# Agent attention: scores laid out with pixels on partitions, one softmax shift for each half of the image

## Chip, cores and metric

The kernel runs on one core of a Trainium2 chip. The metric is the device time of one execution in microseconds (us); for the kernel before it is the median of three runs.

## The reference

Four residual layers act on `x` of shape 32 x 192 x 56 x 56, each on the group-normalised input. The first is the one that changes, an attention through 49 agents with 6 heads of 32 channels. For each image, with n = 3136 pixels:

```python
qkv = xf @ Wqkv + bqkv                       # q, k, v: n x 192
agent = q averaged over a 7 x 7 grid          # 49 x 192
agent_attn = softmax(agent @ k.T * scale + pos_bias, axis=pixels)   # per head: 49 x n
agent_v = agent_attn @ v                                            # per head: 49 x 32
q_attn = softmax(q @ agent.T * scale + agent_bias, axis=agents)     # per head: n x 49
out = (q_attn @ agent_v + depthwise_3x3(v)) @ proj_w + proj_b
```

The change concerns `agent_attn` and `agent_v`: a softmax over all pixels of an image, for each of 6 x 49 = 294 pairs of head and agent. The other three layers (a bidirectional WKV recurrence, a fractional shift, a long convolution through spectra) follow and are not touched.

## The kernel before

`all_blocks` first makes the filter of the last layer, then runs `attention` over the 32 images, then the WKV layer (`scan_pairs`) and the last two layers (`channel_blocks`). Everything is float32.

`attention` cuts an image into four pieces j = 0 to 3, strips of 16, 16, 16 and 8 columns (`WIDTHS`). A piece has two halves (upper and lower rows) of n = 448 pixels (224 in the last), which are again cut into `ns` = 4 (2) subs of 112 pixels (`SUB`). `xs_a` and `xs_c` hold the normalised channels of a piece with channels on partitions; rows 64 to 124 of `xs_c` hold constants that multiply the coefficients of the position bias, so that a score is two matmuls into one PSUM tile. `gk_a` and `gk_c` are the agents seen through the key weights (294 columns), `gq_a` and `gq_c` the same for the second softmax. All PSUM tiles of the attention come from one pool of four, of two banks each.

The work on an image, in the order of the program text:

1. For each piece: `weigh` computes the scores with agents on partitions, one tile of 98 x 2 x 448 for each of three pairs of heads (lines 659 and 660). VectorE takes the highest of a row, negated, into `low` (line 661), and ScalarE applies the exponential from PSUM into `pr` with that shift and adds up the denominators `sums` (line 663). `turn_v` transposes v on TensorE; `turn` transposes `pr` back to pixels on partitions into `prT` (lines 691 and 694), since the product with v sums over pixels. `gather` multiplies `prT` by v (line 706), and `settle` (lines 715 to 719) transposes that result to agents on partitions, into `got`. `find_v` and `convolve` (the depthwise convolution: one ScalarE instruction and eight VectorE instructions on each of two tiles, line 646) of later pieces stand between these. `moments` takes the statistics of the next image.
2. `join` brings the four pieces, each with its own shift, to one, divides by the denominators and yields `values`.
3. A loop over t works through the second softmax: `ask` (scores with pixels on partitions, lines 751 and 752; highest over the 49 agents, exponential, sum, division on VectorE and ScalarE, lines 755 to 768), `turn_back` (transposes, line 778), `answer` (line 791 onward), `project` (output weights and residual), with the next image's statistics, agents, first `find_v` and `convolve` between them. `ask(0)` stands before `join`, so that PE has work there.

A scheduler orders the instructions of each engine from this text, so the order on an engine can differ a little from it. Each engine then works strictly in its order. GpSimd (POOL) has nothing to do in the attention loop of the kernel before.

Of the kernel before, what the change touches and what calls it, by code (L numbers as in the profile page):

```python
# [20 lines left out]
F32 = mybir.dt.float32  # L21
I32 = mybir.dt.int32
AF = mybir.ActivationFunctionType
# [414 lines left out]
def attention(ctx: ExitStack, tc: tile.TileContext, a, ready, x1, st_a, st_c, beside):  # L438
# [15 lines left out]
    mm = nc.tensor.matmul  # L454
    UP, LOW = slice(0, 64), slice(64, 128)
    HALVES = ((0, UP), (1, LOW))
    P2 = slice(0, PAIR)

    def psum():
# [13 lines left out]
    gk_c, gq_c, xs_c = ready.gk_c, ready.gq_c, ready.xs_c  # L473

    NK = len(WIDTHS)
    xs_a = [cp.tile([128, S * w], F32, name=f"xs_a{j}", tag=f"xs_a{j}") for j, w in enumerate(WIDTHS)]


# [12 lines left out]
    def small(name, shape):  # L491
        return sp.tile(shape, F32, name=name, tag=name)
# [14 lines left out]
    def moments(x):  # L507

        st_a, st_c = small("st_a", [128, 7, 6]), small("st_c", [128, 4, 6])
        flat = [t.rearrange("p y x -> p (y x)") for t in x]  # L510
        for i in range(7):
            nc.vector.bn_stats(st_a[:, i], flat[0][:, i * 448 : (i + 1) * 448])
        for i in range(4):
            nc.vector.bn_stats(st_c[:, i], flat[1][:, i * 392 : (i + 1) * 392])
        mv = small("mv", [128, 2, 2])
        nc.vector.bn_aggr(mv[:, 0], st_a.rearrange("p a b -> p (a b)"))
        nc.vector.bn_aggr(mv[:, 1], st_c.rearrange("p a b -> p (a b)"))
        pool_a, pool_c = small("pool_a", [128, AG]), small("pool_c", [65, AG])
        by_x = [wp.tile([128, n, POOL], F32, name="by_x", tag=f"by_x{n}", bufs=1) for n in (S, S // 2)]
        for t in range(2):  # L520
            nc.vector.tensor_reduce(
                by_x[t].rearrange("p y q -> p (y q)"), x[t].rearrange("p y (q x) -> p (y q) x", x=8), AX.X, ALU.add
            )
        nc.vector.tensor_reduce(
            pool_a.rearrange("p (w q) -> p w q", w=POOL), by_x[0].rearrange("p (w y) q -> p w q y", y=8), AX.X, ALU.add
        )
        fours = small("fours", [64, 2 * POOL, POOL])
        for h, r in HALVES:
            nc.vector.tensor_reduce(
                fours[:, h * POOL : (h + 1) * POOL], by_x[1][r].rearrange("p (w y) q -> p w q y", y=4), AX.X, ALU.add  # L530
            )
        nc.vector.tensor_tensor(
            pool_c[0:64].rearrange("p (w q) -> p w q", w=POOL), fours[:, 0::2], fours[:, 1::2], ALU.add
        )
        nc.vector.memset(pool_c[64:65], 1.0)
        return mv, (pool_a, pool_c)
# [45 lines left out]
    def seen(ag, w, to_c, name):  # L582

        ps = psum()
        for i, cols in enumerate((slice(0, 128), slice(128, C + 1))):
            n = (128, 65)[i]
            mm(ps[:n, i, : 4 * AG], w[0][:, cols], ag[0], start=True, stop=True)
            mm(ps[:n, i, 4 * AG : HA], w[1][:, cols], ag[1], start=True, stop=True)
        g = small(name, [128, HA])
        nc.scalar.copy(g, ps[:, 0, :HA])  # L590
        c = sp.tile([65, HA], F32, name="once", tag="once", bufs=1)
        nc.scalar.copy(c, ps[0:65, 1, :HA])
        nc.sync.dma_start(out=to_c[0:65], in_=c.unsqueeze(1).to_broadcast([65, 2 * NK, HA]))
        return g
# [53 lines left out]
        return o  # L648


    def weigh(j, g, low, sums):
        _, n, _ = sizes(j)
        prs = []
        for p in range(3):
            cols = slice(p * PAIR, (p + 1) * PAIR)
            ps = psum()
            for h in range(2):
                px = slice(h * n, (h + 1) * n)
                mm(ps[P2, h, :n], g[:, cols], xs_a[j][:, px], start=True, stop=False)  # L659
                mm(ps[P2, h, :n], gk_c[0:KC, 2 * j + h, cols], xs_c[j][0:KC, px], start=False, stop=True)  # L660
            nc.vector.tensor_reduce(low[:, j, p : p + 1], ps[P2, :, :n], AX.XY, ALU.max, negate=True)  # L661
            pr = wp.tile([PAIR, 2, CH], F32, name="pr", tag="weights", bufs=5)
            nc.scalar.activation(  # L663
                pr[:, :, :n], ps[P2, :, :n], AF.Exp, bias=low[:, j, p : p + 1], accum_out=sums[:, j, p : p + 1]
            )
            prs.append(pr)
        return prs

    def turn_v(j, v):

# [8 lines left out]
            nc.scalar.copy(vT[:, s0 : s0 + 2], ps[:SUB, :, : 3 * 128])  # L679
        return vT  # L680

    def turn(j, prs):

        _, _, ns = sizes(j)
        prT = wp.tile([SUB, 8, HA], F32, name="prT", tag="turned", bufs=2)
        for q in range(0, 2 * ns, 2):
            ps = psum()
            for i in range(2):
                h, s = divmod(q + i, ns)
                for p in range(3):  # L690
                    nc.tensor.transpose(
                        ps[:SUB, i, p * PAIR : (p + 1) * PAIR], prs[p][:, h, s * SUB : (s + 1) * SUB], ident[P2, P2]
                    )
            nc.scalar.copy(prT[:, q : q + 2], ps[:SUB, :, :HA])
        return prT

    def gather(j, prT, vT):

        _, _, ns = sizes(j)
        ps = psum()  # L700
        for p in range(3):
            cols = slice(p * PAIR, (p + 1) * PAIR)
            for s in range(ns):
                for h, r in HALVES:
                    c = h * 128 + p * 64 if p < 2 else 256 + h * 64
                    mm(ps[r, 0, cols], vT[:, s, c : c + 64], prT[:, h * ns + s, cols], start=(s == 0), stop=(s == ns - 1))
        halves = wp.tile([128, HA], F32, name="halves", tag="halves", bufs=1)
        nc.scalar.copy(halves, ps[:, 0, :HA])
        return halves

# [10 lines left out]
    def join(low, sums, got):  # L721

        m = small("m", [PAIR, 3])
        nc.vector.tensor_reduce(m, low.rearrange("p j a -> p a j"), AX.X, ALU.min)
        f = small("f", [PAIR, NK, 3])
        nc.vector.tensor_tensor(f, m.unsqueeze(1).to_broadcast([PAIR, NK, 3]), low, ALU.subtract)
        nc.scalar.activation(f, f, AF.Exp)
        nc.vector.tensor_tensor(sums, sums, f, ALU.mult)
        den = small("den", [PAIR, 3])
        nc.vector.tensor_reduce(den, sums.rearrange("p j a -> p a j"), AX.X, ALU.add)  # L730
        nc.vector.reciprocal(den, den)
        nc.vector.tensor_tensor(f, f, den.unsqueeze(1).to_broadcast([PAIR, NK, 3]), ALU.mult)
        by_pair = got.rearrange("p j (a d) -> p (j a) d", a=3)
        nc.vector.tensor_tensor(
            by_pair, by_pair, _bc(f.rearrange("p j a -> p (j a)"), [PAIR, NK * 3, 2 * HD]), ALU.mult
        )
        values = small("values", [PAIR, 3, 2 * HD])
        nc.vector.tensor_reduce(values.rearrange("p a d -> p (a d)"), got.rearrange("p j c -> p c j"), AX.X, ALU.add)
        nc.vector.tensor_tensor(values, values, heads.unsqueeze(1).to_broadcast([PAIR, 3, 2 * HD]), ALU.mult)
        return values  # L740


    def ask(j, g):
        _, _, ns = sizes(j)
        pq = wp.tile([SUB, 8, HA], F32, name="pq", tag="turned", bufs=2)
        for q0 in range(0, 2 * ns, 4):
            for q in range(q0, q0 + 4, 2):
                ps = psum()
# [22 lines left out]
    def turn_back(j, pq):  # L771
        _, n, ns = sizes(j)
        out = []
        for p in range(3):
            ps = psum()
            for q in range(2 * ns):
# [1 line left out]
                nc.tensor.transpose(  # L778
                    ps[P2, h, s * SUB : (s + 1) * SUB], pq[:, q, p * PAIR : (p + 1) * PAIR], ident[:SUB, :SUB]
                )  # L780
            t = wp.tile([PAIR, 2, CH], F32, name="pqT", tag="weights", bufs=5)
            nc.scalar.copy(t[:, :, :n], ps[P2, :, :n])
            out.append(t)
        return out
# [43 lines left out]
    gk = seen(ag, wkT, gk_c, "gk_a")  # L828
    for j in range(NK):
        normed(nxt, rs, nb, j)  # L830
    v, o = {0: find_v(0), 1: find_v(1)}, {}
    o[0] = convolve(0)
    for b in range(NB):
        x, more = nxt, b + 1 < NB
        if more:
            nxt = ready.image(nc, a, b + 1)
        beside(b)
        low, sums = small("low", [PAIR, NK, 3]), small("sums", [PAIR, NK, 3])
        got = sp.tile([PAIR, NK, C], F32, name="got", tag="got", bufs=1)
        turned, asked, back = {}, {}, {}  # L840
        for j in range(NK):
            prs = weigh(j, gk, low, sums)
            if j == 0:
                gq = seen(ag, wqT, gq_c, "gq_a")
            vT = turn_v(j, v[j])
            if j > 0:
                halves = gather(j - 1, *turned[j - 1])
            if j + 2 < NK:
                v[j + 2] = find_v(j + 2)
            turned[j] = turn(j, prs), vT  # L850
            if j > 0:
                settle(j - 1, halves, got)
            if j + 1 < NK:
                o[j + 1] = convolve(j + 1)
            elif more:
                mv, pools = moments(nxt)
        halves = gather(NK - 1, *turned[NK - 1])
        asked[0] = ask(0, gq)
        settle(NK - 1, halves, got)
        values = join(low, sums, got)  # L860
        done, o = o, {}
        st = small("st", [128, 2, 9])
# [1115 lines left out]
```

## Time and profile before

| | us |
|---|---|
| median of 3 runs (10781.03 to 10796.38) | 10793.86 |
| time of the profiled execution | 10811.08 |
| span of the profiled execution | 10809.3 |
| `values` of the first and of the last image (start of its last instruction) | 278.1 and 4932.4 |
| busy over the span: PE, VectorE, ScalarE, POOL | 9604.3, 9260.0, 6372.8, 2918.0 |

The attention occupies roughly the first 5000 us. PE is TensorE's matmul, DVE is VectorE, ACT is ScalarE. A float32 matmul shows as two records, a transpose as one. A duration of a record includes its start and its way through the pipeline, so instructions that follow each other closely overlap by some 0.08 us on DVE; on PE the distance from start to start is the price of an instruction in a dense sequence.

### The profile page before, as it was taken

To read this page: it belongs to the slowest core of one execution; us is meant where nothing else is said; L and a number is where in the kernel's file an instruction comes from. 1 tells how busy PE (TensorE), PEld (TensorE's weight loads), DVE (VectorE), ACT (ScalarE), POOL (GpSimd) and SP (SyncE) were. 2 spreads that over 40 slices of the span, in tenths; PEclk is the share of its full clock that TensorE was granted. 3 is DMA by queue.
4 is the path that set the end of the run, shared out by engine and by line. 5 is a ranking of instruction groups with operands and counts; after the bars stand their busy time and mean duration, and the time that the engine had idled before them with its cause. 6 is when DMAs were issued, how large, how long until landed. Compare 5 with 4: busy or idle time off the path is not lost. (4 is left out here: it accounts for less than half of the span.)

```text
span 10809.3 us, 166766 instructions
## 1 busy us (share of the span) xinstructions
PE 9604.3 (89%) x64806; PEld 5959.0 (55%) x64806; DVE 9260.0 (86%) x11668; ACT 6372.8 (59%) x11964; POOL 2918.0 (27%) x2614
## 2 busy tenths in 40 slices
PE   6999999999999999998888888888888799999998
PEld 3555555555555555554333333333333577787876
DVE  5888888888888888887999999999999577777877
ACT  3555555555555555554666666666666466666766
POOL 0000000000000000002655555555555444444441
PEclk8999999999999999998999999999999899999999
DMA  4211221112121111111344333333444589999998
GB/s 122 63 47 49 63 64 63 37 58 63 64 63 35 61 46 46 46 34 56 92 102 98 97 97 97 97 97 97 97 101 103 153 269 273 274 275 273 278 274 264
DMA packets 1104877, 1240.31 MB, mean 115 GB/s; under 512 B 773091, under 2 KB 807200, under 8 KB 1091992
## 3 DMA queue, kind: packets, MB, share of 16 engines
q1 hardware_dynamic: 1083148, 1201.53, 38.8%
q10 hardware_dynamic: 20932, 28.02, 1.0%
q8 instruction: 516, 8.45, 0.3%
q14 instruction: 281, 2.30, 0.1%
HBM read 915.94 MB, written 306.43 MB: 113 GB/s over the span
## 5 line engine op out<-in xcount | busy, mean ns | idle before, releaser
L646 DVE SCALAR_TENSOR_TENSOR o<-v_a,att_w,o 128x896 f32<-128x896 f32 (+1 forms) x1024 | 1053.3, 1029 | 421.7 <-ACT v_a L620 296.6
L1163 POOL MEMSET f<- 128x1 f32 x96 | 8.8, 98 | 4842.7 <-DMA st_c<-st 4837.7
L1543 DVE STREAM_TRANSPOSE z<-turned 128x1792 f32<-128x1792 f32 x192 | 677.4, 3528 | 258.3 <-ACT turned L1543 257.8
L1543 ACT COPY y<-ps 64x252 f32<-64x252 f32 (+1 forms) x2304 | 784.0, 340 | 157.9 <-PE ps L1543 128.1
L1156 ACT ACTIVATE q<-q 128x784 f32<-128x784 f32 x384 | 328.3, 855 | 813.6 <-DVE q L1151 638.5
L663 ACT ACTIVATE pr<-ps,low 98x896 f32<-98x896 f32 (+1 forms) x384 | 352.3, 918 | 567.8 <-DVE low L661 567.8
L911 PE MATMUL ps<-sq,fixed 128*128 128x392 f32 x512 | 296.8, 742 | 427.7 <-ACT sq L1234 427.7
L764 ACT ACTIVATE pq<-pq 112x1176 f32<-112x1176 f32 x224 | 265.3, 1184 | 683.3 <-DVE pq L756 654.1
L751 PE MATMUL ps<-gq_a,xs_a 128*112 128x294 f32 x1792 | 609.0, 422 | 46.6 <-DVE pq L756 24.1
L1543 POOL TENSOR_TENSOR xn<-x,scale 128x896 f32<-128x896 f32 x192 | 328.4, 1711 | 1192.3 <-DMA x<-x 759.4
L646 DVE SCALAR_TENSOR_TENSOR o<-v_c,att_w,o 128x448 f32<-128x448 f32 (+1 forms) x1024 | 634.3, 619 | 7.5 <-ACT v_c L631 2.4
L659 PE MATMUL ps<-xs_a,gk_a 128*98 128x448 f32 (+1 forms) x1536 | 638.9, 497 | 0.0
L660 PE MATMUL ps<-xs_c,gk_c 125*98 125x448 f32 (+1 forms) x1536 | 631.3, 492 | 0.0
L911 PE MATMUL ps<-x,weights 128*128 128x392 f32 x1536 | 573.7, 516 | 31.1 <-DVE bv L1185 14.1
L752 PE MATMUL ps<-gq_c,xs_c 125*112 125x294 f32 x1792 | 581.4, 411 | 0.0
L1543 PEld LDWEIGHTS ps<-toep,y 128*32 128x32 f32 x16896 | 508.2, 151 | 113.4 <-ACT y L1543 109.2
L1543 PE MATMUL ps<-toep,y 128*32 128x112 f32 x16896 | 554.8, 287 | 0.0
L1543 PE MATMUL ps<-rows,xn 128*112 128x112 f32 x3072 | 378.5, 281 | 159.6 <-POOL xn L1543 136.0
L1543 ACT ACTIVATE turned<-ps,rs 128x448 f32<-128x448 f32 (+1 forms) x576 | 384.4, 668 | 203.4 <-PE ps L1543 195.7
L1543 PE MATMUL ps<-fixed,padded 128*128 128x168 f32 x3072 | 490.0, 314 | 0.0
L766 DVE TENSOR_REDUCE sm<-pq 112x24 f32<-112x1176 f32 x224 | 307.7, 1374 | 181.9 <-ACT pq L764 181.9
L1543 PEld LDWEIGHTS ps<-fixed,padded 128*128 128x128 f32 x3072 | 455.6, 195 | 2.4 <-issue 1.9
(367 smaller groups left out, 25548.6 us busy)
## 6 DMA issues: line engine op xcount, KB each, us to landing
toep<-spans SPq DMA_DIRECT2D x192, 2352.0 KB
x<-x SPq DMA_DIRECT2D x576, 392.0 KB
x<-x SPq DMA_DIRECT2D x896, 196.0 KB
out_x<-done SPq DMA_DIRECT2D x384, 196.0 KB
spans<-lags SPq DMA_DIRECT2D x24, 2352.0 KB
x<-in_x SPq DMA_DIRECT2D x32, 1568.0 KB
x<-x SPq DMA_DIRECT2D x32, 1568.0 KB
x<-in_x SPq DMA_DIRECT2D x64, 392.0 KB
```

Of the source, the lines that this page charges most:

```text
L646: nc.vector.scalar_tensor_tensor(dst, tap(i), dww[:, t, i : i + 1], dst, ALU.mult, ALU.add)
L659: mm(ps[P2, h, :n], g[:, cols], xs_a[j][:, px], start=True, stop=False)
L660: mm(ps[P2, h, :n], gk_c[0:KC, 2 * j + h, cols], xs_c[j][0:KC, px], start=False, stop=True)
L663: nc.scalar.activation(pr[:, :, :n], ps[P2, :, :n], AF.Exp, bias=low[:, j, p : p + 1], accum_out=sums[:, j, p : p + 1])
L751: mm(ps[:SUB, i, :HA], xs_a[j][:, px], g, start=True, stop=False)
L752: mm(ps[:SUB, i, :HA], xs_c[j][0:KC, px], gq_c[0:KC, 2 * j + (q + i) // ns], start=False, stop=True)
L764: nc.scalar.activation(flat, flat, AF.Exp)
L766: nc.vector.tensor_reduce(sm, rows, AX.X, ALU.add)
L911: mm(out, aa, srcs[t][h], start=True, stop=False)
L1156: nc.scalar.activation(den, den, AF.Ln)
L1163: nc.gpsimd.memset(s, 0.0)
L1543: return lambda *args, **kw: self.tc.keep_in_program_order(do(*args, **kw))
```

## The change

The scores of the first softmax are computed with pixels on partitions, as `ask` does for the second (`score`), and copied by ScalarE into SBUF tiles `sc` of 112 x 8 x 294 (4 x 294 for the last piece). These tiles have the memory that `prT` and `pq` had, now three of the large kind and one of the small. No transposes of exponentials are needed (`turn` is gone). The shift is now one for each half image (pieces 0 and 1, pieces 2 and 3): `highest` takes the maximum over the subs of two pieces on VectorE, `top` transposes that on TensorE and takes the maximum across what were partitions into `low`; `apart` is a diagonal form of it, and `lower` spreads it over 112 partitions with a matmul against ones, subtracts it from all scores of the half image on VectorE, in place, and takes the exponential on ScalarE, in place. `fold` adds the exponentials over subs on GpSimd into `side`, and `add_up` adds `side` over partitions with a matmul into `sums`. `gather` runs over two pieces in one accumulation, so that `settle` runs twice for an image and `join` works on two parts. `tops`, `side`, `halves` and the row sums of `moments` share the buffers of `pqT` (three in place of five).

The diff, cut to its core:

```diff
-    def weigh(j, g, low, sums):
...
-            for h in range(2):
-                px = slice(h * n, (h + 1) * n)
-                mm(ps[P2, h, :n], g[:, cols], xs_a[j][:, px], start=True, stop=False)
-                mm(ps[P2, h, :n], gk_c[0:KC, 2 * j + h, cols], xs_c[j][0:KC, px], start=False, stop=True)
-            nc.vector.tensor_reduce(low[:, j, p : p + 1], ps[P2, :, :n], AX.XY, ALU.max, negate=True)
...
-            nc.scalar.activation(
-                pr[:, :, :n], ps[P2, :, :n], AF.Exp, bias=low[:, j, p : p + 1], accum_out=sums[:, j, p : p + 1]
...
+    def score(j, g):
...
+        for q in range(0, 2 * ns, 2):
+            ps = psum()
+            for i in range(2):
+                px = slice((q + i) * SUB, (q + i + 1) * SUB)
+                mm(ps[:SUB, i, :HA], xs_a[j][:, px], g, start=True, stop=False)
+                mm(ps[:SUB, i, :HA], xs_c[j][0:KC, px], gk_c[0:KC, 2 * j + (q + i) // ns], start=False, stop=True)
+            nc.scalar.copy(sc[:, q : q + 2], ps[:SUB, :, :HA])
+        return sc
+    def highest(parts):
+        tops = wp.tile([SUB, 2, HA], F32, name="tops", tag="weights", bufs=WB)
+        for i, (j, sc) in enumerate(parts):
+            n = 2 * sizes(j)[2]
+            nc.vector.tensor_reduce(tops[:, i], sc[:, :n].rearrange("p q c -> p c q"), AX.X, ALU.max)
+        nc.vector.tensor_tensor(tops[:, 0], tops[:, 0], tops[:, 1], ALU.max)
+        return tops
+    def fold(parts):
...
+        nc.gpsimd.tensor_tensor(side[:, 0:2], t[:, q : q + 2], u[:, r : r + 2], ALU.add)
+        for t, q in rest[2:]:
+            nc.gpsimd.tensor_tensor(side[:, 0:2], side[:, 0:2], t[:, q : q + 2], ALU.add)
+        nc.gpsimd.tensor_tensor(side[:, 0], side[:, 0], side[:, 1], ALU.add)
+        return side
+    def top(i, side, low):
...
+            nc.tensor.transpose(ps[P2, 0, p * SUB : (p + 1) * SUB], side[:, 0, p * PAIR : (p + 1) * PAIR], ident[:SUB, :SUB])
+        nc.vector.tensor_reduce(
+            low[:, i], ps[P2, 0, : 3 * SUB].rearrange("p (a n) -> p a n", a=3), AX.X, ALU.max, negate=True
+        )
+        apart = sp.tile([PAIR, 3, PAIR], F32, name="apart", tag="apart", bufs=1)
+        nc.vector.tensor_tensor(
+            apart, ident[P2, P2].unsqueeze(1).to_broadcast([PAIR, 3, PAIR]), _bc(low[:, i], [PAIR, 3, PAIR]), ALU.mult
+        )
+        return apart
+    def lower(parts, apart):
+        ps = psum()
+        mm(ps[:SUB, 0, :HA], ones[P2, :SUB], apart.rearrange("p a b -> p (a b)"), start=True, stop=True)
+        for j, sc in parts:
...
+            nc.vector.tensor_tensor(
+                sc[:, :n], sc[:, :n], ps[:SUB, 0, :HA].unsqueeze(1).to_broadcast([SUB, n, HA]), ALU.add
             )
...
+            nc.scalar.activation(flat, flat, AF.Exp)
+    def add_up(i, side, sums):
+        ps = psum()
+        for p in range(3):
+            mm(ps[P2, 0, p : p + 1], side[:, 0, p * PAIR : (p + 1) * PAIR], ones[:SUB, 0:1], start=True, stop=True)
+        nc.vector.tensor_copy(sums[:, i], ps[P2, 0, 0:3])
...
-    def turn(j, prs):
...
+        sc[0] = score(0, gk)
+        gq = seen(ag, wqT, gq_c, "gq_a")
+        sc[1] = score(1, gk)
+        tops = highest([(j, sc[j]) for j in range(2)])
+        for j in range(2):
+            vT[j] = turn_v(j, v[j])
+        v[2] = find_v(2)
+        o[1] = convolve(1)
+        apart = top(0, tops, low)
+        sc[2] = score(2, gk)
+        lower([(j, sc[j]) for j in range(2)], apart)
+        v[3] = find_v(3)
+        o[2] = convolve(2)
+        sc[3] = score(3, gk)
+        side = fold([(j, sc[j]) for j in range(2)])
+        halves = gather([(j, sc[j], vT[j]) for j in range(2)])
+        add_up(0, side, sums)
+        tops = highest([(j, sc[j]) for j in range(2, 4)])
+        for j in range(2, 4):
+            vT[j] = turn_v(j, v[j])
+        settle(0, halves, got)
+        o[3] = convolve(3)
+        apart = top(1, tops, low)
         asked[0] = ask(0, gq)
-        settle(NK - 1, halves, got)
+        lower([(j, sc[j]) for j in range(2, 4)], apart)
+        if more:
+            mv, pools = moments(nxt)
+        side = fold([(j, sc[j]) for j in range(2, 4)])
+        halves = gather([(j, sc[j], vT[j]) for j in range(2, 4)])
+        add_up(1, side, sums)
+        settle(1, halves, got)
         values = join(low, sums, got)
```

## Prediction

> **What bounds the kernel now.** I read the busy shares, then the period of an image from the rows of `values`, then one image cut into two stretches. The last instruction of `values` starts at 278.1 in the first image and at 4932.4 in the last, so 31 periods take 4654.3 us, 150.1 us an image, 4803 us for 32. Only this part changes; the remaining 6000 us stay.
>
> ```profile
> PE 9604.3 (89%) x64806; PEld 5959.0 (55%) x64806; DVE 9260.0 (86%) x11668; ACT 6372.8 (59%) x11964; POOL 2918.0 (27%) x2614
> ...
> L739 DVE TENSOR_TENSOR values<-values,att_k x32: 282/346/352, 278.1 to 4932.4; 98x192 f32<-98x192 f32 x32
> ...
> core 0: us, PE busy (x) PEld busy (x) DVE busy (x) ACT busy (x) POOL busy (x), PEclk, DMA share, GB/s
> 2090.80:2157.60 66.80, 63.54 (x301) 37.36 (x301) 50.02 (x77) 41.55 (x67) 0.00 (x0) 0.92 0.05 10
> 2157.60:2241.70 84.10, 80.05 (x508) 51.39 (x506) 77.39 (x116) 39.56 (x78) 0.00 (x0) 1.00 0.28 94
> ```
>
> The two stretches are one image: from its predecessor's `values` to the first score matmul (stretch B, the loop over t), and from there to its own `values` (stretch A, where everything that the change touches lies). The reader should see that PE bounds both, and that in A DVE is close behind: 77.4 of 84.1 us. Whatever lightens PE there can win 6.7 us an image at most, and whatever adds more than that to DVE makes A longer even if DVE never waits.
>
> The groups of the attention, by form, over 28 images (500 to 4700 us), and the neighbours among them that price the new instructions:
>
> ```profile
> line engine op names shapes xcount | busy us, mean ns | idle before us <-releasers
> L661 DVE TENSOR_REDUCE low<-ps 98x1 f32<-98x896 f32 x252 | 268.6, 1084 | 6.6 <-PE ps L660 5.7
> L661 DVE TENSOR_REDUCE low<-ps 98x1 f32<-98x448 f32 x84 | 51.2, 610 | 0.0
> L766 DVE TENSOR_REDUCE sm<-pq 112x24 f32<-112x1176 f32 x196 | 269.2, 1374 | 162.1 <-ACT pq L764 162.1
> L738 DVE TENSOR_REDUCE values<-got 98x192 f32<-98x768 f32 x28 | 40.5, 1447 | 0.0
> L524 DVE TENSOR_REDUCE pool_a<-by_x 128x49 f32<-128x392 f32 x28 | 23.6, 843 | 0.0
> L768 DVE TENSOR_TENSOR pq<-pq,sm 112x1176 f32<-112x1176 f32 x196 | 269.4, 1374 | 1.6
> L764 ACT ACTIVATE pq<-pq 112x1176 f32<-112x1176 f32 x196 | 232.1, 1184 | 610.9 <-DVE pq L756 585.8 <-DVE f L732 24.3
> L694 ACT COPY prT<-ps 112x588 f32<-112x588 f32 x392 | 230.0, 658 | 12.8 <-PE ps L691 11.5
> ```
>
> L738 is the row to look at: it takes longer for 768 elements than L766 for 1176. Both are sums along the free dimension, but L766 reads neighbours, L738 steps 192 elements.
>
> **PE, per image.** From the timeline, a float32 matmul of 448 columns costs 0.755 us from start to start (2158.41, 2159.17, 2159.92), one of 224 0.38, one of 294 0.497, and 24 transposes of L691 2.2. Away go 36 x 0.755 + 12 x 0.38 = 31.7 of scores, 84 transposes of 0.093 = 7.8, and two `settle` of 0.4. In come 56 x 0.497 = 27.8 of scores, two spreading matmuls (1.0), six transposes of `tops` and six matmuls of `add_up` (together 1.6). The balance is -9.9 us, all in A: PE falls to 70 us there.
>
> **ACT, per image.** Fourteen copies of `prT` (0.66) become fourteen copies of `sc` of the same shape. Twelve exponentials with accumulator reads, 13.4 us, become four: L764 and L663 (896 elements, 1011 ns) give 0.83 ns an element behind 0.2 us, so 2.16 for 2352 elements and 1.2 for 1176, 7.7 together. Two `halves` and `got` copies go. ACT has half of A free, so the 7 us count for nothing; without that cover they would be a gain.
>
> **DVE, per image.** Away: L661 11.4 us (319.8 / 28), two additions of L719 (0.6), and half of L738 and of the scaling of `got` (1.05): 13.05. In come:
> - Four reductions of `highest`, over 8 (4) scores that lie 294 elements apart. Here a rule and a row differ. L738 and L524 (steps of 192 and 7) cost 1.69 and 1.77 ns an element behind 0.15 us; at 1.7, 2352 elements take 4.15 us and 1176 take 2.15: 14.3 for the image when 0.08 of overlap is taken off each. The Trainium skill, "VectorE: DVE Perf Modes", section "The perf-mode tier table", gives `tensor_reduce` one rate, 1x, with no condition on its step; its 0.96 GHz and L766's start give 2.6 and 1.38 us, so 8.8. I take the row; the rule would make the sum 5.5 us smaller. The other end is 2.15 ns an element (the dearest stepped row near, `fours` of 196 elements in 486 ns, start included), 3.5 us more.
> - Four additions of `lower` of 2352 and 1176 elements: L768 has 1176 in 1374 ns, so 2.6 and 1.37, 8.85 dense.
> - Two maxima of 294, two `apart`, two `low` (336 elements from PSUM), at 0.36, 0.36 and 0.42 dense, between L719 (192, 0.34) and L755 (588, 0.76); two tiny copies of `sums`: 2.5.
>
> 25.6 in, 13.05 out: +12.6. DVE needs 90.0 us in A where A lasted 84.1. PE's 9.9 us are therefore worth nothing, and DVE sets A.
>
> **Waits on DVE in A.** I walk the order of the changed program as built, with time 0 at the first score matmul. (1) Two pieces are scored before their maximum: 2 x 7.95 us with `seen` (1.6) between. DVE's remaining convolution and residual work of the image before ends at 6.7, the first piece is copied at 8.7, its reduction ends at 12.8; the second piece is copied at 18.3, and nothing stands between the two reductions on DVE. Waits 2.0 + 5.5 = 7.5 us. (2) Then DVE is dense: second reduction, statistics, thirteen taps with `low` and `apart`, the two `lower` additions to 43.5. PE waits for `apart`, and later for exponentials, which costs nothing. (3) In the second half image the order on DVE is `lower`, `lower`, one division by sums, then the copy of `sums`, then `join`. That copy waits for `add_up`, which waits for `fold` on POOL: six additions behind the first exponential. POOL's rows are 421 ns for 112 elements and 1692 for 896, so 1.19 + 0.08 between for 588, 0.8 for the last of 294: 7.15 us. From the end of the first addition: exponential 2.2, fold 7.15, PE 0.5, 9.9 us; DVE has 2.8 of work. Wait 7. Queued behind it are `join`, all `answer`s and `ask(1)`. On PE `ask(1)` stands behind `add_up` too. (4) The first fold (8 additions, 9.7 us) has 11.7 us of taps beside it on DVE, and would be hidden.
>
> **The lock.** Those taps read two operands from SBUF. What that does beside POOL shows in the last layers:
>
> ```profile
> L1543 DVE TENSOR_TENSOR padded<-x,mean x192: 1061/1081/2403, 8522.2 to 10734.8; 128x896 f32<-128x896 f32 x192
> ...
> L1543 POOL TENSOR_TENSOR xn<-x,scale x192: 1682/1692/2536, 8475.0 to 10662.3; 128x896 f32<-128x896 f32 x192
> ...
> L1150 POOL COPY f<-p 128x1 f32<-128x1 f32 x192 | 344.8, 1796 | 315.2 <-DVE p L1149 307.2
> ```
>
> Min, median, max: mostly the two miss each other, and then nothing is lost; where they meet, one takes 1.3 us longer. A copy of one column lasts 1.8 us on POOL beside DVE's two-operand scans. The median row alone would price the lock at nothing; the Trainium skill, "SBUF — State Buffer", section "Who interferes with whom", says that a DVE instruction with two SBUF inputs and a POOL instruction that reads SBUF exclude each other for a whole instruction, which speaks against this change: eight additions, 7 x 1.19 + 0.72 = 9 us of DVE standing still. The bounds are 0 and about 15 (POOL kept out until the taps end, then waited for); I take 9, since the maxima show whole instructions lost and the taps are dense.
>
> **Sum.** A: 90.0 + 7.5 + 7 + 9 = 113.5, +29.4 over 84.1. B stays bound by PE; `ask(1)` is computed after `add_up` and not before `values`, so B starts with PE some 2.5 us late (at most 5, at least 0). +31.9 an image, x 32 = +1021. Against the profiled execution: 10811 + 1021 = 11832; that execution was 17 us above the median, so 11815. No DMA is added or moved past another on SP's queue: `seen` still loads `gq_c` long before `ask(0)`. Three buffers for `pqT` in place of five cost nothing, as `answer` frees them on PE ahead of the next transposes; if a copy did wait, up to 1 us on each of four pieces.
>
> **Rivals.** *The lock costs nothing*: the first fold hides as in (4). A 104.5, +22.9 with B: x 32 = +733, 11527. For: the median row; against: its maximum. *POOL is kept out and stepped reads are dear*: +3.5 and +6 more, 41.4 an image, 12120. For: one copy in the scan took 3.55 us. *DVE reads at the contiguous rate and fills its waits*: 84.5 us in A; if the reductions overlap other work and POOL's sums arrive early, A is 84.5 or slightly less and the time is 10800, not slower; it turns at 84.1 us of DVE time and waits in A. If the waits in B shrank too by the 3 us PE has free there, 10700. For: the rule on `tensor_reduce`; against: L738, and a wait that the order as built contains. That the change doesn't do what it says is excluded by that order.
>
> **Numbers.** Main case with its spread 0.60, no lock 0.20, POOL kept out 0.13, not slower 0.07. A range of 11430 to 12120 leaves out about 2 in 10. 0.2% of this time, 22 us, is about what a measurement can tell from no change: faster by more 0.04, same 0.03, slower 0.93.
>
> **What would show it.** Reductions into `tops` of 4.15 us (2.6 would be the rule); `side` additions of 1.2 us in the second fold, longer in the first, and taps above 1.15 us beside them; DVE idle some 5.5 us before the second reduction and some 7 before the copy of `sums`, released by PE; PE busy about 73% in the attention; `values` every 182 us. A period under 160 us would make the walk wrong, one of 150 the whole argument.

## The result

The changed kernel takes 11951.42 us (median of four, 11944.33 to 11968.09) against 10795.12 us before (four, 10781.03 to 10803.1): a ratio of 1.1075, 95% interval 1.1056 to 1.1094. It is 1156 us slower where 1020 were forecast, and inside the range that was stated (11430 to 12120). The profiled execution has a span of 11947.9 us.

The profile after, in the views that the prediction used: the busy line of the page, the row of `values`, and one image cut in two (from its first score matmul to its `values`, A; from there to the next first score matmul, B; PEclk is the clock that TensorE was granted, 1.00 being full speed).

```profile
PE 9611.3 (80%) x63142; PEld 6121.3 (51%) x63142; DVE 9733.2 (81%) x11732; ACT 6224.5 (52%) x11196; POOL 3802.3 (32%) x3063
...
L781 DVE TENSOR_TENSOR values<-values,att_k x32: 357/358/359, 294.3 to 6068.2; 98x192 f32<-98x192 f32 x32
...
core 0: us, PE busy (x) PEld busy (x) DVE busy (x) ACT busy (x) POOL busy (x), PEclk, DMA share, GB/s
2437.30:2558.00 120.70, 77.89 (x430) 56.02 (x429) 91.16 (x118) 35.25 (x54) 27.42 (x14) 0.77 0.20 65
2558.00:2627.30 69.30, 67.30 (x329) 38.17 (x327) 51.45 (x78) 41.21 (x67) 0.00 (x0) 0.98 0.04 10
```

(6068.2 - 294.3) / 31 = 186.3 us an image, where it was 150.1. Nearly all of the loss is in A, 120.7 us for 84.1; B has 69.3 for 66.8. No engine is busy for 120 us in A: VectorE works 91.2 and stands for 29.5. What it stands for, first as a list of waits (total us, times, longest) between 500 and 5800 us, then in the order of one image, and under it GpSimd in the same stretch:

```profile
DVE sums L721 <- PE ps L720: 531.8, 49, 12.3
DVE tops L676 <- ACT sc L668: 204.7, 57, 5.5
...
2446.21 4.18 DVE L676 TENSOR_REDUCE tops<-sc 112x294 f32<-112x2352 f32 x1 [1.79 <-ACT sc L668]
2455.85 4.27 DVE L676 TENSOR_REDUCE tops<-sc 112x294 f32<-112x2352 f32 x1 [5.46 <-ACT sc L668]
2504.93 0.16 DVE L721 COPY sums<-ps 98x3 f32<-98x3 f32 x1 [12.30 <-PE ps L720]
2554.97 0.16 DVE L721 COPY sums<-ps 98x3 f32<-98x3 f32 x1 [9.33 <-PE ps L720]
...
2483.87 10.03 POOL L686 TENSOR_TENSOR side<-sc 112x588 f32<-112x588 f32 x1 [118.57 <-ACT sc L715]
2493.98 8.91 POOL L688 TENSOR_TENSOR side<-side,sc 112x588 f32<-112x588 f32 x6
2502.98 0.70 POOL L689 TENSOR_TENSOR side<-side 112x294 f32<-112x294 f32 x1
2545.17 1.75 POOL L686 TENSOR_TENSOR side<-sc 112x588 f32<-112x588 f32 x1 [41.49 <-ACT sc L715]
2547.01 5.94 POOL L688 TENSOR_TENSOR side<-side,sc 112x588 f32<-112x588 f32 x4
```

The wait ahead of `sums` is put down to PE, but PE only passes on what GpSimd finished 1.25 us earlier (2503.68). The same kind of addition takes 10.03 us at 2483.87 and 1.75 at 2545.17. The first of them starts inside VectorE's taps and ends 1.3 us after the last of those, about what one addition takes, and the taps beside it have their usual length:

```profile
2490.88 1.15 DVE L649 SCALAR_TENSOR_TENSOR o<-v_a,att_w,o 128x896 f32<-128x896 f32 x1
2491.94 0.69 DVE L649 SCALAR_TENSOR_TENSOR o<-v_c,att_w,o 128x448 f32<-128x448 f32 x1
2504.93 0.16 DVE L721 COPY sums<-ps 98x3 f32<-98x3 f32 x1 [12.30 <-PE ps L720]
```

In the last eight images, which have no `beside` copies, the scheduler puts `moments` behind the second `lower`. The second wait is covered there and the period is 179 us, where it is 189 in the mean of the images before. The trace thus holds a first test by itself.

### The profile page after: what moved, and what is told of

Read it like the earlier page. It is cut to its first block, busy times and chain, and to the rows that moved or that the text cites. A ratio compares the mean times of both kernels' runs of the same rounds, so it can differ in the third digit from the quotient of the medians.

```text
span 11947.9 us, 163456 instructions
## 1 busy us (share of the span) xinstructions
PE 9611.3 (80%) x63142; PEld 6121.3 (51%) x63142; DVE 9733.2 (81%) x11732; ACT 6224.5 (52%) x11196; POOL 3802.3 (32%) x3063
## 5 line engine op out<-in xcount | busy, mean ns | idle before, releaser
L686 POOL TENSOR_TENSOR side<-sc 112x588 f32<-112x588 f32 x64 | 377.2, 5894 | 4995.1 <-ACT sc L715 4995.1
L649 DVE SCALAR_TENSOR_TENSOR o<-v_a,att_w,o 128x896 f32<-128x896 f32 (+1 forms) x1024 | 1064.4, 1039 | 238.1 <-ACT o L647 129.4
L793 PE MATMUL ps<-gq_a,xs_a 128*112 128x294 f32 x1792 | 696.1, 480 | 103.2 <-DVE low L697 103.1
L676 DVE TENSOR_REDUCE tops<-sc 112x294 f32<-112x2352 f32 (+1 forms) x128 | 471.7, 3708 | 225.3 <-ACT sc L668 225.3
L649 DVE SCALAR_TENSOR_TENSOR o<-v_c,att_w,o 128x448 f32<-128x448 f32 (+1 forms) x1024 | 646.4, 631 | 3.1 <-ACT v_c L634 0.9
L745 PE MATMUL ps<-sc,vT 112*64 112x98 f32 x5376 | 330.6, 295 | 391.1 <-ACT sc L715 390.4
L794 PE MATMUL ps<-gq_c,xs_c 125*112 125x294 f32 x1792 | 639.9, 447 | 0.0
L666 PE MATMUL ps<-gk_a,xs_a 128*112 128x294 f32 x1792 | 622.2, 429 | 0.0
L667 PE MATMUL ps<-gk_c,xs_c 125*112 125x294 f32 x1792 | 606.2, 420 | 0.0
L745 PEld LDWEIGHTS ps<-sc,vT 112*64 112x64 f32 x5376 | 308.7, 172 | 428.1 <-ACT sc L715 417.4
L793 PEld LDWEIGHTS ps<-gq_a,xs_a 128*112 128x112 f32 x1792 | 356.1, 207 | 288.7 <-DVE low L697 124.7
```

Source lines behind the costliest of these rows:

```text
L649: nc.vector.scalar_tensor_tensor(dst, tap(i), dww[:, t, i : i + 1], dst, ALU.mult, ALU.add)
L666: mm(ps[:SUB, i, :HA], xs_a[j][:, px], g, start=True, stop=False)
L667: mm(ps[:SUB, i, :HA], xs_c[j][0:KC, px], gk_c[0:KC, 2 * j + (q + i) // ns], start=False, stop=True)
L676: nc.vector.tensor_reduce(tops[:, i], sc[:, :n].rearrange("p q c -> p c q"), AX.X, ALU.max)
L686: nc.gpsimd.tensor_tensor(side[:, 0:2], t[:, q : q + 2], u[:, r : r + 2], ALU.add)
L745: mm(ps[r, 0, cols], vT[:, s, c : c + 64], sc[:, h * ns + s, cols], start=(k == 0), stop=(k == len(steps) - 1),)
```

## Experiments

Times are medians; ratios are to the kernel before on the same chip. The table gives one middle image of each kernel: A and B, VectorE's busy time in A, and that of the 53 instructions of the taps in A (L649; L646 before the change, L652 in the last row but one). It cuts at the start of the last instruction of `values`, the lines above at its end, 0.4 us later.

| kernel | time, us | ratio (95%) | A / B, us | DVE busy in A | taps in A |
|---|---|---|---|---|---|
| before | 10795 | | 84.4 / 67.1 | 77.7 | 38.1 |
| changed | 11951 | 1.1075 (1.1056-1.1094) | 120.3 / 69.7 | 90.8 | 37.7 |
| no fold | 11386 | 1.0551 (1.0528-1.0574) | 103.5 / 67.1 | 90.6 | |
| late sums, first try | 11763 | 1.0904 (1.0881-1.0926) | 113.9 / 69.4 | | |
| one-input taps | 11781 | 1.0918 (1.0895-1.0941) | 114.9 / 69.4 | | |
| maxima without a step | 11903 | 1.1029 (1.1004-1.1053) | 118.7 / 69.1 | | |
| late sums | 11647 | 1.0801 (1.0782-1.0820) | 112.0 / 68.9 | 91.5 | 37.7 |
| three edits | 11587 | 1.0740 (1.0723-1.0758) | 112.1 / 66.6 | 96.5 | 39.8 |
| sums by TensorE | 11986 | 1.1107 (1.1089-1.1126) | 121.3 / 69.3 | 90.7 | 37.7 |
| no shift, no fold | 10613 | 0.9843 (0.9827-0.9860) | 82.8 / 61.5 | 69.3 | 37.5 |
| no shift, fold late, `moments` last | 10793 | 1.0005 (0.9996-1.0015) | 88.4 / 61.7 | 77.1 | 45.6 |
| no shift, fold late | 10817 | 1.0021 (1.0013-1.0030) | 88.6 / 61.6 | 77.2 | 45.3 |
| no shift, `v` early | 10897 | 1.0093 (1.0077-1.0110) | 90.4 / 61.7 | 82.6 | 50.8 |
| no shift, fold in place | 10852 | 1.0058 (1.0042-1.0075) | 88.8 / 62.9 | 77.5 | 45.7 |

**No fold.**

```
-    (fold's additions)
+    return parts[0][1]
```

> The additions on GpSimd are left out: the denominator matmuls read the exponentials of the first sub of a half image in place of the folded sums, so the denominators lack all other subs. Everything else stays. Theory (both waits before the copies of the sums are GpSimd's, 12.3 us in 31 images and 9.3 in 24): the first wait goes whole, since the gather on TensorE ends before the taps do; of the second some 4.5 us stay for the last exponentials and the gather. 12.3 x 31 + 4.8 x 24 = 496 us less, 11455. Rival (GpSimd only stands last in a chain that is as long without it, through exponentials and gather): less than 100 us gained, 11850 or more.

11385.91 us, 566 less than the changed kernel and 69 below the theory's number. The waits ahead of `sums` fall from 531.8 us to

```profile
DVE sums L713 <- PE ps L712: 113.8, 22, 5.2
```

between 500 and 5500 us. So about half of the loss hangs on GpSimd; the other half, 591 us, is there without it.

**Late sums, first try.** `add_up(0)` moves behind the second `lower`; to make room, `apart` moves into the ring of buffers that `side` uses.

```
-    apart = sp.tile(..., tag="apart", bufs=1)
+    apart = wp.tile(..., tag="weights", bufs=WB)
-    add_up(0, side, sums)          # behind the first gather
+    add_up(0, first, sums)         # behind the second lower
```

> Nothing is left out: the matmuls that add up the first half image's denominators, and the copy of their sums, stand behind the second half image's spreading of the shift (its folded sums in a small tile of their own; the diagonal tile shares the rotating buffers). GpSimd works as before, held or not. Theory (the first wait exists only because TensorE and VectorE stand in order behind the first fold): it goes, 12.3 x 31 = 381 us, 11570; the second wait stays in the first 24 images. Rival (GpSimd's operations take VectorE's time itself, so that the time comes back as longer taps or reductions): 11850 or more, with two-operand taps longer than 1.16 us in the median.

11763.39 us. The first wait is gone, but my own edit put another in its place, `apart` waiting for a buffer that the delayed fold still holds:

```profile
DVE sums L722 <- PE ps L721: 200.8, 22, 9.3
...
DVE apart L702 <- POOL folded L690: 153.5, 27, 5.7
```

**Late sums.** The same, with `apart` in the unused half of `tops`.

> Nothing of the computation is left out: the denominators of the first half are read only behind the second `lower`, and `apart` lies in the unused half of the tile of maxima, so that it takes no buffer from the side tiles. Theory (the first reading of `sums` in the order of VectorE is a wait of 12.3 us that is paid in full): with the wait gone and no new one in its place, 24 to 31 of the images lose 12.3 us each, 300 to 380 us in all, so 11570 to 11650 us. Rival (VectorE's later instructions wait for something else in that stretch, the second scores or `v`, and the stall only moves): 11850 us or more, and a new wait of 6 to 12 us under the maxima or the taps.

11646.72 us, 305 less, inside the theory's range. GpSimd's first addition is held as long as ever, but nobody on VectorE reads its sum yet. A smaller new wait is left, up to 3.3 us an image for the buffer that the fold still holds (69.9 us in 21 images). The fold's additions:

```profile
2566.17 10.45 POOL L686 TENSOR_TENSOR side<-sc 112x588 f32<-112x588 f32 x1 [118.94 <-ACT sc L716]
2576.70 19.95 POOL L688 TENSOR_TENSOR side<-side,sc 112x588 f32<-112x588 f32 x6
```

**One-input taps.** The 16 taps of the third piece are replaced by row maxima of the same input, so that they read one operand from SBUF; the outer taps of that piece's convolution are left out of its result.

```
+    if j == 2:
+        nc.vector.tensor_reduce(junk[:, :rows], tap(i), AX.X, ALU.max)
```

> In the convolution of the third piece the eight multiply-adds on each tile become maxima along a row, of the same elements and of nearly the same duration (1.08 and 0.6 us): one operand from SBUF in place of two. That convolution's eight outer taps are left out of the output. Theory (two-operand instructions on VectorE, one behind the other, keep GpSimd's first addition out): the first addition of the first fold takes 1.4 to 2.5 us in place of 9.4 to 11, the fold ends some 8 us earlier, and 8 x 31 = 250 us go, 11700. Rival (the first addition is slow for a reason of GpSimd's own, such as waking after 118 us of idleness): it stays near 10 us and the time at 11950.

11781.25 us, 170 less: between the two, nearer the theory. The page's row of first additions, both folds together, in the changed kernel (5894 ns each) and here:

```profile
L686 POOL TENSOR_TENSOR side<-sc 112x588 f32<-112x588 f32 x64 | 377.2, 5894 | 4995.1 <-ACT sc L715 4995.1
```

```profile
L690 POOL TENSOR_TENSOR side<-sc 112x588 f32<-112x588 f32 x64 | 104.0, 1625 | 5103.1 <-ACT sc L719 5103.1
```

The first fold is held no more. Its first addition and the copy of its sums in one image:

```profile
2430.48 1.43 POOL L690 TENSOR_TENSOR side<-sc 112x588 f32<-112x588 f32 x1 [119.03 <-ACT sc L719]
2443.79 0.16 DVE L725 COPY sums<-ps 98x3 f32<-98x3 f32 x1 [6.83 <-PE ps L724]
```

GpSimd was idle for 119 us here too, and the exponential is the same, so neither of these held it: the unbroken run of taps did. Two-operand taps of the last piece still stand between the reductions, and do not keep it out there. The first wait falls from 12.3 to 6.8 us; 5.5 x 31 = 170 is the whole gain. It does not go because the edit also moved instructions: ten of the sixteen reductions lie behind the copy of `sums` now, and VectorE has less to do ahead of it. The second wait, 9.3 us, is still paid.

A reduction also writes less than a tap, 56 elements for 896, so this run alone does not tell whether the second operand counts or the writing. The WKV layer of the changed kernel's own trace does. VectorE's `bv` reads one operand from PSUM and one from SBUF and writes 784 elements; 129 one-column copies on GpSimd lie beside it alone, and each takes 0.18 or 0.19 us. The scans, with their operands in SBUF, keep such a copy waiting until they end:

```profile
7296.44 0.96 DVE L1239 TENSOR_TENSOR bv<-ps,ek 128x784 f32<-128x784 f32 x1
7296.74 0.18 POOL L1198 COPY p<-b 128x1 f32<-128x1 f32 x1
...
7310.73 1.82 DVE L1203 TENSOR_TENSOR_SCAN q<-decay,b,ek 128x784 f32<-128x784 f32 x1
7310.87 1.66 POOL L1204 COPY b<-p 128x1 f32<-128x1 f32 x1
```

Together the two say that it is the second operand from SBUF that keeps GpSimd out.

**Maxima without a step.** Each reduction over eight scores becomes two-input maxima of 588 neighbours.

```
-    nc.vector.tensor_reduce(tops[:, i], sc[:, :n].rearrange("p q c -> p c q"), AX.X, ALU.max)
+    nc.vector.tensor_tensor(tops, tops, t[:, q : q + 2], ALU.max)
```

> Nothing is left out: the maximum over subs is taken with two-operand maxima of 588 neighbouring elements (seven for the first half image, five for the second, and one of 294) in place of reductions that step over 294 elements. Theory (the stepped reductions cost 4.2 and 2.1 us because of the step, and stand on VectorE's path): 8.5 us become 5.2 in the first half, most of it already done when the last scores come, and 6.5 become 3.8 in the second: 5.5 to 6 us an image, 180 us, 11770. Rival (reductions hide in waits that stay): within 40 us of 11950.

11902.99 us, 48 less of the 180 hoped for. The maxima take 0.77 us each, but in the first half they run into the scores (waits of 2.9 us ahead of them), the sums are waited for as before (12.3), and a new wait of 3.5 us for `got` follows. Cheaper reductions mostly turned into waiting: that is the rival, if a little beyond its 40 us.

**Three edits at once**: late sums, maxima without a step, and `moments` behind the second gather.

> Nothing of the computation is left out. Three edits to the changed kernel at once: sums of the first half read behind the second `lower`; maxima by 588-wide two-input instructions without a step; `moments` of the next image set behind the second gather, so that it lies in the second wait for `sums`. Theory (two waits for GpSimd's sums are the largest idle stretches of VectorE, and both can be covered): 12.3 + 9.3 us less in 24 images, some 12 in the others, and up to 3 us from the maxima, so 11,200 to 11,400 us. Rival (VectorE's own work of 91 us sets the stretch whatever the order): not below 11,550 us. Neither is as fast as the kernel before, since 91 us of VectorE's work stand against 80 of TensorE there.

11586.5 us; the rival's bound holds and the theory fails. Both waits ahead of `sums` are gone from the list, but VectorE's work in A is 96.5 us. Some 5 us of the second softmax's work moved from B into A, and two-operand instructions beside the fold are longer: the taps take 39.8 us for 37.7, the two `apart` 2.1 for 0.9. Smaller waits add up beside it: 6.8 us an image for scores, 5.4 for `mx` (3.8 in the changed kernel), 3.7 for a buffer that the fold holds, 3.6 for `answer`. A is the 112 us of the late sums alone; the gain over them lies in B.

**Sums by TensorE.** One-column matmuls over all blocks of pixels, accumulated in PSUM, in place of GpSimd's fold.

```
+    for n, s in enumerate(side):
+        mm(ps[P2, 0, p : p + 1], s[:, p * PAIR : (p + 1) * PAIR], ones[:SUB, 0:1], start=(n == 0), stop=(n == len(side) - 1))
```

> Nothing of the computation is left out: the denominators are added by TensorE, with 48 and 36 one-column matmuls in PSUM in place of 6 and GpSimd's fold. Theory (what the fold costs is the wait for GpSimd, and TensorE has over 40 us free in the stretch): both waits ahead of `sums` go but for some 5 us, as in the run without the fold, and the matmuls (some 0.19 us each, by 1.15 us for six) hide: 11,390 to 11,480 us. Rival (78 more matmuls of a column lie on the way to `values`, 9 and 7 us that replace the waits): 11,700 us or more.

11985.93 us: the theory fails, and the rival is right in kind. These are two chains of one image on TensorE (last column: idle before, and for what), and VectorE's reading behind each; in most images the second wait is longer still, 14.7 us:

```profile
2514.24 3.59 PE L738 MATMUL ps<-sc,vT 112*64 112x98 f32 x80
2517.76 9.12 PE L713 MATMUL ps<-ones,sc 112*98 112x1 f32 x80
...
2567.10 4.79 PE L738 MATMUL ps<-sc,vT 112*64 112x98 f32 x72 [11.71 <-ACT sc L707]
2571.82 7.28 PE L713 MATMUL ps<-ones,sc 112*98 112x1 f32 x72
...
2526.91 0.16 DVE L714 COPY sums<-ps 98x3 f32<-98x3 f32 x1 [8.03 <-PE ps L713]
2579.13 0.16 DVE L714 COPY sums<-ps 98x3 f32<-98x3 f32 x1 [11.55 <-PE ps L713]
```

A matmul of one column costs 0.10 to 0.11 us (7.28 / 72, 9.12 / 80), and the profile counts two for each float32 product, 168 of them an image. They stand behind the gather, whose start in the second chain waits for the exponentials. So I read the wait as one of place as well as of cost: where `sums` stands in VectorE's order is early for either engine that adds behind the exponentials, and the engine sets the size.

**No shift, no fold.** The exponential is taken from PSUM; the highest, the subtraction and the fold are left out.

```
-    nc.scalar.copy(sc[:, q : q + 2], ps[:SUB, :, :HA])
+    nc.scalar.activation(sc[:, q : q + 2], ps[:SUB, :, :HA], AF.Exp)
```

> Left out: the subtraction of the highest score (maxima, `apart`, `lower`), and the denominators' sum over the blocks of pixels. The exponential is taken on the way out of PSUM; the new layout with pixels on partitions, its gathers and its transposes of `v` stay. Theory (the layout is cheap and its price lies in the maxima, the subtraction and the fold): VectorE's work in the stretch from the first score to `values` falls by 25 us to about 65 us, TensorE bounds both stretches with 72 to 76 and 67 us, and an image takes 140 to 143 us, so about 10,500 us, below the kernel before. Rival (the layout itself costs, by its transposes and by gathers with 49 or 64 columns at a time): 10,900 us or more.

10612.61 us, 1.6% faster than before the change. The layout with pixels on partitions is not what costs. One image, A and B, then the head of B in the kernel before and here:

```profile
2360.79:2443.62 82.83, 70.48 (x453) 51.79 (x451) 69.30 (x108) 28.75 (x50) 0.00 (x0) 0.92 0.29 96
2443.62:2505.12 61.50, 58.62 (x295) 32.21 (x294) 46.66 (x77) 40.25 (x67) 0.00 (x0) 1.00 0.05 11
...
2091.61 1.83 PE L542 MATMUL ps<-mv,att_k 128*128 128x1 f32 x8 [3.09 <-DVE pq L756]
...
2442.97 0.95 PE L545 MATMUL ps<-mv,att_k 128*128 128x1 f32 x8
```

TensorE's saving in A is there, 70.5 us of work for 80.1, but A itself is only 1.6 us shorter. Most of the gain is in B, 61.5 us for 67.1 with nearly the same work: in the kernel before, TensorE stands 3.1 us for VectorE at its head and then works at half rate (84 transposes add up to 26.9 us, here to 22.0). The theory had 72 to 76 for A and 67 for B; it came out 110 us too low. In A VectorE now stands 11 us an image ahead of its statistics for the load of the next image (307.5 us in 28 images), a wait that neither the kernel before nor the changed one has. That this wait is what keeps A above 76 us is likely, but no run takes it away alone.

**No shift, fold late** (once with `moments` behind the second gather, once at its old place).

> Left out: only the subtraction of the highest score, which cancels in the quotient as long as no exponential overflows; the denominators are still added by GpSimd, the first half's are read late, and `moments` lies behind the second gather. Theory (the fold costs nothing where its wait is covered, and the subtraction and the maxima are what made VectorE the bound): within 100 us of the kernel that leaves both out, some 10,500 to 10,650 us. Rival (GpSimd's additions still hold up the end of the second half): 10,900 us or more, with a wait of 7 us or more ahead of the second reading of `sums`.

> Left out: only the subtraction of the highest score (the highest itself, `apart`, `lower`). As the run before of that kind, but with `moments` of the next image at its old place. In that run VectorE stood 9.2 us ahead of the statistics, for the load of the next image, and the 10 us of the pools lay between the last gather and `values`. Theory (that place of `moments`, and not GpSimd's fold, made it 180 us slower than the kernel without subtraction and fold): within 60 us of the latter, 10,600 to 10,670 us. Rival (the fold costs that much even where its sums are read late): 10,740 us or more.

10792.82 and 10817.29 us: both theories missed by some 145 us, and the place of `moments` is not the reason. These two don't price the fold, though: I had given `folded` one buffer for both halves, so the second fold's last addition waits for the first one's reading (the line is from the run with `moments` at its old place). Their taps (45.6 and 45.3 us) already show what the last run does.

```profile
2368.98 0.71 POOL L690 TENSOR_TENSOR folded<-side 112x294 f32<-112x294 f32 x1 [16.65 <-PE ps L721]
```

**No shift, `v` early**: `find_v(2)` ahead of the second piece's scores, and the statistics tied behind the third piece's taps.

> Left out: only the subtraction of the highest score. Two more edits: `v` of the third piece is made ahead of the second piece's scores, and the statistics of the next image are tied behind the third piece's taps by a small copy, so that VectorE meets neither the load of the next image (9 us) nor the wait for `v`. Theory (with the subtraction gone, the stretch from the first score to `values` is bound by VectorE's standing in wait, not by work): 72 to 78 us for that stretch and 62 for the other, 134 to 140 us an image, so 10,280 to 10,470 us. Rival (the end of the stretch, the last fold and its sums behind the last scores, is what sets it): 10,560 us or more.

10896.74 us, slower than without these edits: the theory fails, and the rival's bound holds, though not for its reason: no wait for `sums` is among VectorE's longest. The wait for the load is gone, but `v` is waited for still (5.9 us at the longest) and the taps take 50.8 us where 37.5 is their own length. It has the same shared `folded`.

**No shift, fold in place.** The run that settles the fold, with the changed kernel's own `fold` and `add_up`.

> Left out: only the subtraction of the highest score (the highest itself, `apart`, `lower`). Everything else as in the changed kernel, GpSimd's fold and both readings of `sums` at their old places included. The two runs of this kind with the late reading held one small tile for both folds; in the traces the second fold's last addition waited 16 to 19 us for the first one's reading, so they don't tell what the fold costs. Theory (without the subtraction the exponentials come straight after the scores, before VectorE's taps fill its queue, so the fold is early and free): within 70 us of the kernel without subtraction and fold, 10,600 to 10,690 us, GpSimd's first addition of a fold not over 4 us and no wait over 2 us ahead of `sums`. Rival (the fold costs some 200 us wherever it lies, by GpSimd and VectorE together): 10,740 us or more.

10851.81 us, 239 above the one without the fold: the rival. GpSimd's additions are short, nothing waits for `sums`, and still A is 6 to 8 us longer. The time is in VectorE's own instructions. GpSimd and VectorE beside the second fold of one image:

```profile
2358.89 1.83 POOL L686 TENSOR_TENSOR side<-sc 112x588 f32<-112x588 f32 x1 [26.23 <-PE ps L757]
2360.80 6.77 POOL L688 TENSOR_TENSOR side<-side,sc 112x588 f32<-112x588 f32 x4
...
2358.76 0.68 DVE L649 SCALAR_TENSOR_TENSOR o<-v_c,att_w,o 128x448 f32<-128x448 f32 x1
2359.35 0.15 DVE L721 COPY sums<-ps 98x3 f32<-98x3 f32 x1
2359.47 1.74 DVE L649 SCALAR_TENSOR_TENSOR o<-v_c,att_w,o 128x448 f32<-128x448 f32 x1
2361.13 0.34 DVE L761 TENSOR_TENSOR got<-got,ps 98x192 f32<-98x192 f32 x1
2361.39 1.58 DVE L649 SCALAR_TENSOR_TENSOR o<-v_a,att_w,o 128x448 f32<-128x448 f32 x1
2362.90 1.62 DVE L649 SCALAR_TENSOR_TENSOR o<-v_c,att_w,o 128x224 f32<-128x224 f32 x1
2364.44 1.84 DVE L649 SCALAR_TENSOR_TENSOR o<-v_a,att_w,o 128x448 f32<-128x448 f32 x1
...
2369.15 0.67 DVE L649 SCALAR_TENSOR_TENSOR o<-v_a,att_w,o 128x448 f32<-128x448 f32 x1
2369.75 0.44 DVE L649 SCALAR_TENSOR_TENSOR o<-v_c,att_w,o 128x224 f32<-128x224 f32 x1
```

Beside the additions a tap of 0.67 us takes 1.58 to 1.84, one of 0.44 takes 1.62. Over the image the 53 taps take 45.66 us where they take 37.51 without the fold: 8.15 us, x 32 = 261, which covers the difference.

No kernel that keeps the whole computation came out faster than the one before; the best of them, the three edits, takes 11587 us. The nearest with complete denominators, 10793 us, has lost the subtraction of the highest and the safety that it gives.

## Why the prediction was right, and where its terms were off

- *VectorE sets A.* Right: 91.2 us of work against 90.0 forecast. Reductions of 4.2 and 2.1 us (4.15 and 2.15), `lower` 2.60 and 1.33 (2.6 and 1.37), `low` 0.42 from start to start (0.42). The row of stepped reductions held; the estimate from the rule on `tensor_reduce` would have put 2.6 where 4.2 was measured. (The 2.15 ns an element of the dear end does not follow from its row: 486 ns for 196 elements are 2.48 with the start, 1.71 without 0.15 us of it. It bears only on a rival.)
- *Waits for scores*, 7.5: measured 1.79 + 5.46 = 7.25.
- *The lock*, 9 us as taps that stand still: the step that failed in form, for this kernel. The taps kept their length (37.7 us, as without any fold); GpSimd was held 10 us and VectorE then waited 12.3. That is the form of the upper bound, "POOL kept out", at a price between the 9 taken and its 15. The sign named for it, taps above 1.15 us, is missing. The one-input taps show the cause; with the fold in place and no shift, the form that I had written down appears, 8.15 us. That 9 us for the wrong form lay only 3.3 below the price of the right one is luck.
- *Wait for the second fold*, 7: measured 9.33, the term of the sum that was mis-sized. An addition of 588 takes 1.42 us, not the 1.19 that I interpolated between rows of 112 and 896, so the fold takes 8.6 us and not 7.15; that accounts for 1.4 of the 2.3 us. TensorE's part, from the end of the fold (2553.72) to the copy of `sums` (2554.97), takes 1.25 us and not 0.5, which is most of the rest. Eight images don't pay this wait, which the walk did not see.
- *B*, 69.3: measured 69.3. `ask(1)` starts late as said, and its first matmuls behind the wait run at half rate (0.98 us from start to start, then 0.50).
- *The sum of A*: 91.2 + 7.25 + 12.3 + 9.33 = 120.1 for 113.5. 186.3 us an image for 182.0, 4.3 x 32 = 138 us, is the distance of 136 us between 11951 and 11815. Two errors partly cancel in it: 6.6 us more in A would be some 211 us over 32 images, and the eight images without the second wait give some 75 back.
- *Rivals.* A free lock (11527) falls with the 12.3 us. "POOL kept out and stepped reads dear" (12120) had the form of the first half right, but the reads came at the price of the row. "Not slower" needed 84.1 us of VectorE's work and waits; there were 120.
- *TensorE's 9.9 us worthless*: so here. Its busy time in A fell only to 77.9 us, where 70 were forecast, at a granted clock of 0.77; that cost nothing, as VectorE sets A. Without shift and fold TensorE's and VectorE's savings together brought 180 us (10792 to 10613), most of it in B.

## What to carry to other kernels

Walk the order of the engine that will be the bound and look for each tiny instruction that reads another engine's result: a copy of three columns cost 12.3 us here because it stood ahead of work that did not need it, and reading it later won 305 us, with two small tiles placed elsewhere to make room. A helper on GpSimd beside taps with two SBUF operands is not free: either it is kept out and its reader waits, or the taps stand still, 8 to 12 us an image in both forms. When an engine's work is made cheaper inside a stretch with waits, count what it will wait for next; two of these experiments, late sums at the first try and the maxima without a step, lost much of their gain to a wait that their own edit made.

## What the runs showed of the hardware

- GpSimd is kept out by VectorE's two-operand instructions beyond one instruction: for 10.03 us, until some eleven of them without a gap had ended. The Trainium skill, "SBUF — State Buffer", "Who interferes with whom", says that whoever issues first holds the pair for a whole instruction; the trace of the last run agrees for a single tap (0.9 to 1.2 us longer beside an addition of 1.42), and that of the changed kernel shows in addition that it isn't always handed over in between. In the late-sums kernel a run of the same taps kept it out again, for 9.20 us in the middle of a fold; in the last run they took turns, and with one-input reductions between the taps the addition took 1.43 us. What decides between the forms stays open.
- A stepped reduction keeps its price when it is long: 4.18 us for 2352 elements 294 apart, 1.7 ns an element.
- TensorE behind a wait runs at half rate for some microseconds: 18 transposes took 4.07 us behind 13.76 us of idleness, 0.226 each, where 24 took 2.79 elsewhere, 0.116 each. The granted clock was 0.67 from 2485 to 2546 us and 1.00 from 2560 to 2620.

```profile
2503.73 1.15 PE L720 MATMUL ps<-ones,side 112*98 112x1 f32 x6 [13.76 <-POOL side L689]
2504.75 4.07 PE L732 MATMUL ps<-att_k,v 128*112 128x128 f32 x18
```
